# Reordering the start of a Mamba-2 decoder layer: first two units in one explicit order, with PE transposes and PE-spread decays

## The chip, the cores and the metric

The kernel runs on one core of a Trainium2 chip. Its time is device time in microseconds from launch to end; the median of several runs is given. A profile of one execution shows when each instruction ran on each engine: TensorE (PE, with its weight loads as PEld), VectorE (DVE), ScalarE (ACT), GpSimd (POOL), and SyncE (SP), which issues most DMAs.

## The reference: what is computed

Sixteen sequences (batches) of 256 positions and 512 features pass one decoder layer: a Mamba-2 block, a linear-attention block over a context, and a feed-forward block with quantised weights and activations. The change lies in the first. Cut to what matters here:

```python
xz = x @ W_in                              # x after LayerNorm; z 2048, xBC 2048+64+64, dt 32
conv = silu(depthwise_conv4(xBC) + b)      # gives x_conv (32 heads of 64), B (64), C (64)
dt = softplus(dt_proj + dt_bias); A = -exp(A_log)
def step(h, (x_t, dt_t, B_t, C_t)):
    dA = exp(A * dt_t)
    h = dA * h + dt_t * x_t * B_t
    return h, (h . C_t) + D * x_t
y = scan(step); y = y * silu(z); y = y * rsqrt(mean(y*y) + eps); out = y @ W_out
```

## The kernel before: tiles, stages and order

**Pairs and units.** Batches are taken two at a time: eight pairs. In a pair, the 2,048 inner features are taken 128 at a time (two heads): 16 units, so 128 slots of one unit each. The kernel never steps through time. For a unit it multiplies the inputs by a 256x256 matrix of decays times C.B per head, tile by tile of 128 positions. The steps of a unit, with their lines:

- `project_part` (L817): z and x of the unit, for both batches, 12 products each of 128x512 in f16 pairs (hi and lo parts of weight and input, L643).
- `silu_z` (L830), `conv_x` (L836), three taps (`tap_of`, L661), `silu_x` (L845).
- `load_decays` and `load_so_far` (L798, L808): the unit's rows of decays are read from DRAM, the same rows to all 128 partitions, 512 KB and 256 KB per unit.
- `scan` (L851): two VectorE scans make running products of the decays; `cross` (L859) makes the off-diagonal tile.
- `times_g` (L868, L872): multiplies these by G, the masked product C.B of the pair.
- `turn_x` and `x_dt` (L880, L890): x transposed on PE and scaled by dt. `scan_out` (L900, L907): the products with the decay tiles. `plus_dx`, `gated` (L915, L920): y.
- one slot later `split_y`, `squares`, `out_product` (L926, L927, L937, L950): y W_out, summed in four PSUM banks over 16 units.

**What a pair needs first.** `norm_transposed` (L561) makes LayerNorm of a batch, splits it into f16 hi and lo and transposes each by DMA (L624). `time_steps` (L666) makes dt and the decays of all heads, transposes them on PE (L723) and stores them to DRAM (L739, L740). `states` (L744) projects B and C, applies convolution and Silu (L758, L661, L766), copies C from partitions 64 to 127 down to 0 to 63 by DMA (L769), and makes G with six products per batch (L777, L782, L786).

**What pair 0 does besides.** Weights arrive in f32. For each unit `scale_units` (L433) squares them on ACT and derives a power-of-two scale from a PE sum and a chain of six small VectorE instructions; `prepare` (L453) scales on VectorE (wzx, L460), casts on ACT and splits on GpSimd (L464). `wout_make` (L505) does the like for W_out. Units 0 to 9 keep their weights in SBUF; units 10 to 15 share two buffers (`keep_w`, L403): they are prepared in pair 0, stored to DRAM, and later streamed back. So pair 0 takes its units in the order `FIRST` (L107).

**Order.** All engines follow an order that the program writes out itself (`manual_schedule`). A preamble (L1711 to L1771) is written by hand: `step(gen, n)` runs a generator to its n-th `yield`, and the instructions in between go to their engines' queues. Then a loop over slots (L1772) places the unit steps, and between them eight points, `advance(now)` (L1626), at which a small planner places the pieces of background tasks. A task's yield names its wait in points, the allowed points, its engine and its cost; tasks are taken by `rank`, lowest first. `plan` (L1663) starts tasks at given slots. PSUM has one bank for such tasks, given out by `Banks`. In the preamble, unit 0's projections follow batch 1's transposes, decays of units 0 and 1 are loaded, unit 0 is scanned; `times_g` of unit 0 and the rest of `states` (from L769 on) come in slot 1 of the loop (L1816 to L1819). The context for the attention block is made by tasks that `plan` starts in slots 6, 8 and 9.

Of the kernel before, what the change touches and what calls it, by code (L numbers as in the profile page):

```python
# [36 lines left out]
F32 = mybir.dt.float32  # L37
# [10 lines left out]
P = 128  # L48
# [10 lines left out]
def decoder_kernel(  # L59
# [47 lines left out]
    FIRST = (14, 15, 0, 1, 2, 3, 12, 13, 4, 5, 6, 7, 8, 9, 10, 11)  # L107
# [88 lines left out]
    with ExitStack() as part:  # L196
# [84 lines left out]
        class Banks:  # L281
# [8 lines left out]
            def take(self, own=False):  # L290
                me = [own]
                self.line.append(me)
# [25 lines left out]
        def misc(hold, shape, name):  # L318
            ps, tag = (ps_m, "m") if hold == "own" else (ps_p, "proj")
            return ps.tile(shape, F32, tag=tag, name=name)  # L320
# [10 lines left out]
        for j in range(3):  # L331
            nc.scalar.dma_start(bq_sb[32 * j : 32 * j + H, :], bq)
        nc.scalar.dma_start(bk_sb[0:H, :], bk)
# [69 lines left out]
        def keep_w(c, loaded=False):  # L403
# [4 lines left out]
            if not loaded:  # L408
                yield landed(6)
                start(clock[0] // POINTS, scale_units(c, c + 2), rank=-2)  # L410
                start(clock[0] // POINTS, prepare(c + 1), rank=-2)
                yield from prepare(c)
# [20 lines left out]
        def scale_units(c0, c1):  # L433
# [5 lines left out]
            yield pe(0.1)  # L439
            hold = yield from bank.take()  # L440
            pt = misc(hold, [P, c1 - c0], f"ss_ps_{c0}")
            nc.tensor.matmul(pt, ones, ssq_zx[:, c0:c1], start=True, stop=True)
            yield dve(1.2)
# [9 lines left out]
        def prepare(c):  # L453
# [7 lines left out]
            yield act(1.0)  # L461
# [13 lines left out]
        def prepare_bcdt():  # L475
# [14 lines left out]
            scales_from(pt, s, inv_bcdt, "bcdt")  # L490
            for k, (w, cols) in reversed(tuple(enumerate(parts))):
# [68 lines left out]

        def norm_transposed(src, b, what, store):  # L561
# [17 lines left out]
            if b < 2 and what == "m":  # L579
                yield  # L580
                nc.gpsimd.tensor_tensor(rs, rs, mhalf[:, 0:NT], ALU.pow)
                yield
                for i in range(NT):
                    nc.vector.tensor_scalar(
                        y[:, i, :], src[:, i, :], mv[:, i, 0:1], rs[:, i : i + 1],
                        ALU.subtract, ALU.mult,
                    )
                yield
            else:
                nc.vector.tensor_scalar(mv[:, :, 1], mv[:, :, 0], -1.0, None, ALU.mult)  # L590
                yield 1, range(POINTS), "pool", 1.5
                nc.gpsimd.tensor_tensor(rs, rs, mhalf[:, 0:NT], ALU.pow)
                nc.gpsimd.tensor_tensor(mv[:, :, 1], mv[:, :, 1], rs, ALU.mult)
                yield act(2.3, 2)
                for i in range(NT):
                    nc.scalar.activation(
                        y[:, i, :], src[:, i, :], AF.Identity,
                        scale=rs[:, i : i + 1], bias=mv[:, i, 1:2],
                    )
            nc.scalar.copy(hi, y)  # L600
            if b < 2 and what == "m":

                yield
                nc.vector.tensor_tensor(lo, y, hi, ALU.subtract)
            else:
                yield pool(2.4)
                nc.gpsimd.tensor_tensor(lo, y, hi, ALU.subtract)
                yield issued()
# [6 lines left out]
            else:  # L615
                if b % 2 == 0:
                    yield from turned.take()
                    store["lnT"] = [
                        p2.tile([P, 2, NT, KD, P], F16, tag=f"lnT_{n}", name=f"lnT_{n}_m_{b}")
                        for n in "hl"  # L620
                    ]
# [10 lines left out]
        def norm_pair(pair):  # L632
            for j in range(2):
                yield from norm_transposed(None, 2 * pair["k"] + j, "m", pair)
# [13 lines left out]
        def project_pair(dst, w, pair, apart=False, between=None):  # L648

            if apart:  # L650
                for j in range(2):
# [1275 lines left out]
```

## Time and profile before

| what | value |
| --- | --- |
| median of 3 runs | 1966.56 us (1964.16 to 1972.84) |
| profiled execution | 1968.45 us, its span 1966.7 us, mean granted TensorE clock 0.973 |
| PE, DVE, ACT, POOL busy | 1812.7, 1648.8, 1241.2, 720.2 us |
| start of the scans (L851) of units in slots 0, 1, 2, 3, 4 | 47.5, 52.2, 84.1, 95.3, 109.9 us |
| of slots 8, 12, 16 (pair 1) | 170.9, 226.6, 275.0 us |
| of slot 127, the last | 1580.7 us |
| pair 1 to 7, mean per slot | 11.76 us |
| DMA | 360.87 MB, mean 183 GB/s |

The span is what the profiler saw from the first to the last instruction; the execution's time holds 1.75 us more. A slot is best followed by the start of its scan on VectorE, because each unit has exactly one pair of them. The "granted clock" is TensorE's clock in parts of full speed. A line of the timeline reads: start, length, engine, line, operation, output<-inputs, shapes, count, and in brackets how long the engine had been idle and what ended that.

### The profile page before, as it was taken

The numbers are of one execution on the slowest core, as the hardware profiler recorded it, in microseconds if no ns is written. First come the engines' busy times: TensorE is split into PE (matmuls) and PEld (weight loads), VectorE is DVE, ScalarE is ACT, GpSimd is POOL, SyncE is SP. The second block draws the span as 40 slices with busy tenths as digits, with TensorE's granted clock in tenths as the row PEclk, the third lists the DMA queues.
The fourth block names the chain that finished last, engine by engine and source line by source line (L and its number), as shares of the span: only waits on it lengthen the run. The fifth ranks groups of instructions, "written<-read, shape, count | busy, mean of one in ns | idle before, by whom it ended". The sixth has DMA issues, their size and how long they took to land.

```text
span 1966.7 us, 29947 instructions
## 1 busy us (share of the span) xinstructions
PE 1812.7 (92%) x10220; PEld 1040.4 (53%) x10220; DVE 1648.8 (84%) x2705; ACT 1241.2 (63%) x2870; POOL 720.2 (37%) x714
## 2 busy tenths in 40 slices
PE   2687998997999999999999999999999988999998
PEld 2344555654566655566556555655565643444443
DVE  5799986876798888788888898788887878999996
ACT  3665665665677566566766666566656547667775
POOL 2365453333324344565456544343323222100000
PEclk9799999998999999999999999999999999999999
DMA  7555576669758768696578778765858825555454
GB/s 226 152 135 174 160 215 180 187 211 212 208 180 243 222 179 241 201 269 187 160 243 253 180 218 227 212 161 175 221 173 228 235 87 111 120 124 110 113 115 91
DMA packets 301826, 360.87 MB, mean 183 GB/s; under 512 B 168101, under 2 KB 202437, under 8 KB 301674
## 3 DMA queue, kind: packets, MB, share of 16 engines
q1 hardware_dynamic: 282794, 298.10, 57.3%
q0 software_dynamic: 18176, 60.83, 8.7%
q8 instruction: 81, 1.33, 0.3%
q14 instruction: 71, 0.58, 0.1%
q10 hardware_dynamic: 704, 0.04, 0.0%
HBM read 280.47 MB, written 39.58 MB: 163 GB/s over the span
## 4 chain that ended last, share of the span: by engine, by line
PE 63%; DVE 19%; ACT 5%; issue 5%; DMA 4%; POOL 3%; SPq 0%; ACTq 0%; POOLq 0%; DVEq 0%
PE pp L643 23%; PE po L950 13%; PE py L900 5%; PE po_f L1525 4%; PE pu L1484 4%; PE pg L1484 4%; DVE m L851 3%; DVE xs L661 3%; PE trx L880 2%; PE py L907 2%; DVE m L868 1%; ACT xdt L890 1%; DMA wchunk<-in_w_gate_t 1%; DMA ln_m<-in_x 1%; DVE h L1489 1%
## 5 line engine op out<-in xcount | busy, mean ns | idle before, releaser
L643 PE MATMUL pp<-lnT_h_m,w 128*128 128x512 f16 (+1 forms) x2064 | 666.1, 384 | 30.1 <-DVE xs L661 21.0
L643 PEld LDWEIGHTS <-w 128*128 128x128 f16 x3096 | 298.4, 100 | 377.0 <-issue 56.3
L927 POOL TENSOR_TENSOR yl<-y,yh 128x512 fp32r<-128x512 f32 x128 | 172.6, 1349 | 712.2 <-ACT yh L926 657.9
L661 DVE SCALAR_TENSOR_TENSOR xs<-pp,convw_sb,xs 128x510 f32<-128x510 f32 (+2 forms) x384 | 286.2, 745 | 171.4 <-ACT xs L836 162.1
L643 PE MATMUL pp<-lnT_l_m,w 128*128 128x512 f16 (+1 forms) x1032 | 396.0, 384 | 0.0
L890 ACT ACTIVATE xdt<-trx,dt 128x64 f32<-128x64 f32 x1024 | 222.6, 327 | 202.1 <-PE trx L880 201.8
L950 PE MATMUL po<-wout,yh 128*128 128x512 f32 x1024 | 336.7, 410 | 0.2 <-DMA wout<-wout_d 0.2
L851 DVE TENSOR_TENSOR_SCAN m<-dab,starts 128x512 f32<-128x512 f32 x256 | 312.9, 1263 | 0.0
L950 PEld LDWEIGHTS po<-wout,yh 128*128 128x128 f32 x1024 | 183.7, 189 | 56.6 <-ACT sq L937 10.9
L950 PE MATMUL po<-wout,yl 128*128 128x512 f32 x512 | 203.6, 398 | 1.8 <-POOL yl L927 1.8
L845 ACT ACTIVATE xs<-xs 128x512 f32<-128x512 f32 x128 | 80.9, 632 | 193.6 <-DVE xs L661 193.6
L900 PE MATMUL py<-m,xdt 128*64 128x256 f32 x1024 | 163.4, 398 | 20.5 <-ACT xdt L890 12.9
L859 ACT ACTIVATE m<-edb,m 128x128 f32<-128x128 f32 x512 | 164.0, 395 | 16.9 <-DVE m L851 16.5
L1484 PEld LDWEIGHTS <-yT 128*128 128x128 bf16 x1024 | 100.4, 99 | 138.1 <-issue 22.4
L836 ACT ACTIVATE xs<-pp,convb_sb,convw_sb 128x512 f32<-128x512 f32 x128 | 100.1, 782 | 108.3 <-PE pp L643 108.2
L938 POOL TENSOR_TENSOR ssq<-ssq,sq 128x512 f32<-128x512 f32 x120 | 155.8, 1298 | 33.5 <-ACT sq L937 32.7
L868 DVE TENSOR_TENSOR m<-m,g 128x1024 f32<-128x1024 f32 x128 | 161.6, 1263 | 0.1
L1484 PE MATMUL pg<-w_ffn,yT 128*128 128x512 bf16 x512 | 133.2, 383 | 8.5 <-ACT h L1488 5.6
L1484 PE MATMUL pu<-w_ffn,yT 128*128 128x512 bf16 x512 | 133.2, 383 | 5.8 <-DVE x L976 5.1
L1488 ACT ACTIVATE h<-pg,sg 128x512 f32<-128x512 f32 x128 | 86.7, 682 | 75.9 <-PE pg L1484 75.7
L1525 PE MATMUL po_f<-w_ffn,hT 128*128 128x512 bf16 x512 | 127.4, 383 | 4.8 <-DMA hT<-hq 4.8
L950 PEld LDWEIGHTS po<-wout,yl 128*128 128x128 f32 x512 | 96.7, 189 | 27.9 <-POOL yl L927 4.6
(261 smaller groups left out, 2856.5 us busy)
## 6 DMA issues: line engine op xcount, KB each, us to landing
dab<-da_d SPq DMA_DIRECT2D x128, 512.0 KB
wout<-wout_d SPq DMA_DIRECT2D x112, 512.0 KB
edb<-ed_d SPq DMA_DIRECT2D x128, 256.0 KB
w<-w_d SPq DMA_DIRECT2D x40, 512.0 KB
w<-in_w_zx SPq DMA_DIRECT2D x16, 512.0 KB
wout_d<-wout SPq DMA_DIRECT2D x16, 512.0 KB
ctxT<-in_ctx_t POOLq DMA_DIRECT2D x16, 512.0 KB, 8.0
x<-in_x SPq DMA_DIRECT2D x16, 512.0 KB
```

What stands on the lines that cost most here:

```text
L643: nc.tensor.matmul(dst, w(wi, kc), yT[yi][:, :, kc, :], start=n == 0, stop=n == 3 * KD - 1)
L661: nc.vector.scalar_tensor_tensor(u[:, :, d:S], raw[:, :, 0 : S - d], w[:, j : j + 1], u[:, :, d:S], ALU.mult, ALU.add,)
L851: nc.vector.tensor_tensor_scan(u["m"][:, 4 * j : 4 * j + 4, :].rearrange("p k t -> p (k t)"), u["da"][:, j].rearrange("p h i t -> p (h i t)"),
L859: nc.scalar.activation(u["m"][:, 8 + n, :], u["ed"][:, n // 2, n % 2, :], AF.Copy, scale=u["m"][:, 2 * n, P - 1 : P],)
L868: nc.vector.tensor_tensor(m, m, gi.unsqueeze(2).to_broadcast([P, 2, 2, NT * P]), ALU.mult)
L890: nc.scalar.activation(u["xdt"][:, j, i, h, :], u["tr"][:, j, i, h * HD : (h + 1) * HD], AF.Copy, scale=dt[:, i, j, 2 * c + h : 2 * c + h ...
L900: nc.tensor.matmul(py[h * HD : (h + 1) * HD, j, :].rearrange("p (i t) -> p i t", i=NT), xdt[:, j, 0, h, :], m[:, 2 * (2 * j + h) : 9 + 2 * ...
L927: nc.gpsimd.tensor_tensor(lo, u["y"], hi, ALU.subtract)
L938: nc.gpsimd.tensor_tensor(pair["ssq"], pair["ssq"], sq, ALU.add)
L950: nc.tensor.matmul(pair["po"][n], u["yhl"][yi][:, j, i * P : (i + 1) * P], w[:, wi, :], start=c == 0 and p == 0, stop=c == NU - 1 and p == 2,)
L1484: nc.tensor.matmul(dst, yT[:, kc, :], w_ffn[w + kc][:, cols], start=kc == 0, stop=kc == KD - 1)
L1525: nc.tensor.matmul(u["po"], u["hT", k // (KF // 2)][:, k % (KF // 2), :], w_ffn[2 * KD + k // NF][:, (k % NF) * D : (k % NF + 1) * D], sta ...
```

## The change

The preamble and slots 0 and 1 are written out in one order, and the loop starts at slot 2. In it:

- Batch 0 is loaded as two tiles. `norm_first` replaces `norm_transposed` for batches 0 and 1: f32 transposes on PE into PSUM, four per tile of 128 positions; hi is cast out of PSUM on ACT, lo subtracted on VectorE.
- `spread_decays`: for unit 0 the decay rows, in SBUF after `time_steps`, are spread over all partitions by PE products with a repeated column of the identity; the DMA loads of unit 0's decays go, those of unit 2 come in their place.
- Unit 1's projections follow unit 0's directly; `states` goes on to the C copy (L769) in the preamble, and G follows before unit 0's `times_g`.
- All ten resident weights are requested before the first LayerNorm; units 0 to 3 get their scales in one chain.
- Four small DMAs of the query and key biases go from ACT's queue to GpSimd's.
- In `plan`: units 12 and 13 move one place back in `FIRST`, unit 4 two places forward; context constants start in slot 10 (before 6), query weights in 14 (8), the first context in 12 (9). Several ranks and waits change. Batch 3 of pair 1 gets a buffer of its own.

The diff, cut to its core:

```diff
-    FIRST = (14, 15, 0, 1, 2, 3, 12, 13, 4, 5, 6, 7, 8, 9, 10, 11)
+    FIRST = (14, 15, 0, 1, 2, 3, 4, 12, 13, 5, 6, 7, 8, 9, 10, 11)
...
-            nc.scalar.dma_start(bq_sb[32 * j : 32 * j + H, :], bq)
-        nc.scalar.dma_start(bk_sb[0:H, :], bk)
+            nc.gpsimd.dma_start(bq_sb[32 * j : 32 * j + H, :], bq)
+        nc.gpsimd.dma_start(bk_sb[0:H, :], bk)
...
+        def norm_first(y, b, pair):
...
+            pts = []
+            for i in range(NT):
+                pt = ps_o.tile([P, KD, P], F32, tag=f"o{NT * b + i}", name=f"ln_t_{b}_{i}")
+                pts.append(pt)
+                for kc in range(KD):
+                    nc.tensor.transpose(pt[:, kc, :], y[:, i, kc * P : (kc + 1) * P], ident)
+                nc.scalar.copy(hi[:, b, i], pt)
+            yield
+            for i in range(NT):
+                nc.vector.tensor_tensor(lo[:, b, i], pts[i], hi[:, b, i], ALU.subtract)
+            yield
...
+        def spread_decays(u):
...
+                    for i in range(NT):
+                        one = 2 * NH * i + row
+                        nc.tensor.matmul(
+                            u["da"][j][:, h, i, :], ident[:, one : one + 1].to_broadcast([P, P]),
+                            pair["da_t"], start=True, stop=True,
+                        )
...
-                start(s, time_steps(pair), rank=-1)
+                start(s, time_steps(pair), rank=-1 if k else -5)
...
-                elif s == 1:
-                    start(s, keep_w(12), rank=-2)
+                elif s == 2:
+                    start(s, keep_w(12), rank=-3)
                 elif s == 7:
-                    start(s, keep_w(10), rank=-2)
+                    start(s, keep_w(10), rank=-3)
...
-                if c == 6:
+                if c == 10:
                     start(s, context_constants())
-                elif c == 8:
+                elif c == 14:
                     start(s, queries_weights(), 1, 2)
-                elif c == 9:
+                elif c == 12:
                     start(s, context_pair(0), 1, rank=1)
...
+        for c in range(NRES):
+            load_w(c)
...
+        step(norm1)
+        step(prep1)
+        pair["ready", "m"] = True
+        project_part(u0, 0, of=0)
+        step(steps_)
+        step(scale1, 3)
+        project_part(u0, 0, of=1)
+        project_part(u0, 1)
...
+        step(steps_, 2)
+        step(scale1, 2)
+        conv_x(u0)
+        step(scale1)
+        step(steps_, 3)
+        step(scale1)
+        step(states_, 2)
+        step(prep2, 2)
+        step(steps_, 3)
+        step(prep2)
+        for n in (1, 2):
+            u = units[n] = units.get(n) or unit(n)
             load_decays(u)
             load_so_far(u)
+        spread_decays(u0)
         silu_z(u0)
-        conv_x(u0)
+        step(states_, 3)
         for j in (2, 1, 0):
             tap(u0, j)
         silu_x(u0)
-        step(states_, 4)
-        step(scales_[1], 5)
+        step(prep2)
+        project_part(u1, 0)
+        plan(0)
+        advance(1)
         scan(u0)
         cross(u0)
-        for s in range(n_slots + 3):
+        turn_x(u0)
+        x_dt(u0)
+        silu_z(u1)
+        advance(2)
+        project_part(u1, 1)
+        conv_x(u1)
+        advance(3)
+        drive(states_)
+        times_g(u0)
+        for j in (2, 1, 0):
+            tap(u1, j)
+        silu_x(u1)
+        plan(1)
+        advance(8)
+        scan_out(u0)
+        scan(u1)
+        cross(u1)
+        advance(9)
+        plus_dx(u0)
+        gated(u0)
...
+        for s in range(2, n_slots + 3):
...
-            if s == 1:
-
-                drive(states_)
-                times_g(u1)
```

## The prediction

> **What bounds the kernel now.** I read the shares of busy time first: TensorE (PE) is busy 92% of the span, so 154 us without a matmul are spread over 1,966.7 us. The 40 slices put the holes at the front. So I took the busy time in stretches (columns: stretch, its length, then PE, PEld, DVE, ACT, POOL busy with instruction counts, granted clock, DMA share, GB/s):
>
> ```profile
> 40.00:50.00 10.00, 0.59 (x2) 0.50 (x2) 5.57 (x12) 4.22 (x9) 0.00 (x0) 0.65 0.56 153
> 50.00:60.00 10.00, 5.42 (x16) 2.78 (x17) 9.89 (x11) 6.92 (x17) 7.39 (x4) 0.50 0.87 215
> 60.00:70.00 10.00, 3.25 (x16) 1.30 (x14) 2.44 (x5) 6.87 (x14) 5.51 (x4) 0.84 0.93 339
> 70.00:80.00 10.00, 6.66 (x31) 5.03 (x32) 6.38 (x15) 0.00 (x0) 1.43 (x3) 0.50 0.14 18
> ...
> 130.00:145.00 15.00, 13.35 (x113) 8.29 (x111) 14.96 (x9) 8.79 (x22) 14.32 (x10) 1.00 0.61 130
> ```
>
> Between 40 and 80 us PE has 15.9 us of work and VectorE 24.3; nothing is full. From 130 on VectorE is. The chain that ended last, in order of time (start, length, what), says what the early stretch waits for:
>
> ```profile
> 61.22 8.64 DMA cT<-bcT
> 69.99 1.63 PE pg L777 x6
> 72.42 1.63 PE pg L777 x6
> 74.69 1.13 DVE m L868
> ```
>
> That is the copy of C to partitions 0 to 63 (L769), the six products C.B per batch (L777), and the first multiplication of decays by them (L868), which every unit needs. Why so late? SyncE's timeline: the decays of units 0 and 1 are asked for at 41.7, C only at 61.2, though its Silu (L766) had ended at 43.64:
>
> ```profile
> 41.69 0.39 SPq L798 DMA_DIRECT2D dab<-da_d  x1
> 42.18 0.41 SPq L808 DMA_DIRECT2D edb<-ed_d  x1
> 42.64 0.46 SPq L798 DMA_DIRECT2D dab<-da_d  x1
> 43.16 0.70 SPq L808 DMA_DIRECT2D edb<-ed_d  x1
> ...
> 61.22 0.59 SPq L769 DMA_DIRECT2D cT<-bcT  x1
> ```
>
> L769 stands in slot 1 behind loads that wait for VectorE. From 82 to 275 us the 14 remaining slots of pair 0 take 13.65 us each (first scan at 84.1, pair 1's at 275.0) against 11.76 later; VectorE is busy 186.2 of the 200 us from 75 to 275. So whatever brings the first L868 forward shifts a full VectorE stretch, and behind it a full PE stretch: it reaches the end one for one unless that stretch gets longer.
>
> **Part 1: LayerNorm turned on PE.** Before, batch 1's hi and lo go through two transposing DMAs: lo is written at 23.25, its DMA issued at 23.28, PE gets it at 26.60, and the time-step products L678 end at 27.4. Now: 16 PE transposes (the row trx x4 is 0.63 us for four; 2.5 us in all), four ACT copies out of PSUM at about 0.65 (L830, 128x512 out of PSUM: 0.69) and four VectorE subtractions at about 0.65 (L604 is 1.23 for twice the width). Batch 1 is normalised at about 18.3 (before 20.5; its statistics follow batch 0's at once), turned by 20, copied by 20.5, split by 21.8. Then 12 products of 256 columns for batch 0 (0.21 each cold, 2.5), of which 1.3 lie ahead of the split, and the 48 of L678 (1.3): 24.7 instead of 27.4, **2.7 gained**. Bounds: nothing, if the ACT queue (now with the weight casts and squares between the copies) is late by as much; 6 if PE is warm and nothing queues. Pushed later in SyncE's order is batch 1's load: before, the ninth DMA (L391) waited until the first (alog) landed at 6.1; now that load is ninth. Half a megabyte at the 390 GB/s of that stretch lands by about 10, its reader comes at 12.9: hidden; uncovered it would cost up to 4. The ten weight loads now issue before 20 us instead of until 28.7; they read in what was idle DMA time and end by about 28.
>
> The Trainium skill ("Advanced Engine Details and Errata", X-Bar Transpose) speaks against this part: a transposing DMA on trn2 is to be as fast as a plain one. The trace agrees: 3.3 us from issue to use here, against a 4.5 us median for the plain 256 KB loads of L508. By the rule the only thing to win is the latency of a DMA, not a slow transpose; the sum above counts just that.
>
> **Part 2: decays by PE.** VectorE's chain L692 to L736 was 8.05 us (27.41 to 35.46). Inserted ahead of its end are one scale chain (1.0) and one wzx (0.75), of which 0.76 fills the wait for the transpose: da_t ends at 35.46 - 2.7 + 1.0 = 33.8. Unit 0's decays then need 12 products instead of a DRAM round trip. No row has such an f32 product with 128 columns and 128 rows; the nearest are L777 (64 rows, 0.14 warm, 0.27 cold) and, from above, L900 (256 columns, half the columns of PE, mean 0.64 cold). So 1.7 to 7.7; I take 3, near L777. The unit 0 scan can run at 38 instead of 47.5, but **it is not on the path**: its reader L868 waits for C. If I am off by all of 4.7, that still ends before C.
>
> The skill ("FP8 and Floating Point Precision", TensorE Precision Notes) counts four passes for a true f32 product, which would be about 2.6 us warm and 5.1 cold for the twelve, as an estimate. Neither moves the sum, for the same reason.
>
> **Part 3: C earlier, unit 1 right behind.** SyncE now has da_d x2, ed_d, then decays of units 1 and 2 (again 2 x 768 KB), then cT. Stores to first load took 35.49 to 41.69, 6.2 us; so loads issue at 33.8 + 6.2 = 40.0 and cT at about 42 (bcT's Silu ends at 36.5, so it does not wait for that). Before, 1.5 MB of broadcasts drained from 42.0 to about 50.2; so they end at 48.3 and cT at 48.5. Bounds: from its own issue plus a 4.5 us median landing, 46.5; plus the 8.64 us of before, 50.6. From there 4.7 us, as before (69.99 to 74.69, at a granted clock of 0.50, which I keep since PE idles from about 42; 3.2 warm by L777's and L782's rows): first L868 at **53.2 instead of 74.6, 21.4 earlier** (bounds 19 to 25).
>
> Then the stretch to slot 2's first instruction (L868 of unit 1, at 82.36 before). Before it held 7.75 us. Now: L868 and L872 of unit 0 (1.8), unit 1's taps (2.3), its scan (2.3, which before lay at 52 to 56), L915 and L920 (1.45), statistics of batch 2 (2.1), one wzx (0.75): 10.7. Slot 2 starts at 53.2 + 10.7 = 63.9: **18.5 earlier**. PE's part of unit 1 (24 products, 0.215 apart warm, 0.42 cold before) lies before 42, under the wait for C.
>
> **Part 4: rest of pair 0.** The same instructions in another order: context constants from slot 6 to 10, query weights 8 to 14, context pairs 9 to 12, units 12 and 13 one slot later, unit 4 earlier. VectorE's sum is unchanged: 0. Context results were written at 452 us, slot 31, and pair 1 asks for them in slot 34; if they miss that, two batches take the store-and-reload path: 2 MB, about 11 us of DMA at the mean 183 GB/s, beside everything else on queues that the page shows 57% and 9% busy. Bounds of part 4 come from VectorE's own rows: the same two scans take
>
> ```profile
> 136.43 5.29 DVE L851 TENSOR_TENSOR_SCAN m<-dab,starts 128x512 f32<-128x512 f32 x2
> ...
> 151.16 2.33 DVE L851 TENSOR_TENSOR_SCAN m<-dab,starts 128x512 f32<-128x512 f32 x2
> ```
>
> and at 136 GpSimd is in unbroken tensor_tensor work (14.32 of 15 us), at 151 it is idle. Mean minus shortest over the stretch: scans 28 x 0.28, L868 16 x 0.20, L920 15 x 0.37, L511 13 x 0.33, L460 10 x 0.40, about 25 us, with single inflated small ones about 35 us that VectorE loses while both run. A new order can raise or lower this by some 10 either way; I have no row that favours a side.
>
> **Sum.** Profiled execution 1,968.45 (1.75 outside its span), less 18.5: 1,950. The median of the runs shown, 1,966.56, lies 1.9 under the profiled one, so **1,948**. Likeliest case alone: 18.5 with -10 to +12 of parts 1, 3 and 4: 1,936 to 1,957.
>
> **Rivals.**
> A, given back at units 10 and 11 (0.14). Their loads wait until unit 13 is used. Before: loaded at 154 (slot 7), GpSimd's split from 242.7, first use on PE at 247.5: 93 us of chain with 2.6 to spare. Unit 13 is now used one slot later while unit 10 stays in slot 14. If the chain stays 93 us, PE waits 13.65 - 2.6 = 11 us: 1,959. Against it: that chain now has a better rank (-3 instead of -2) and the first place at the bank, and 93 us hold only some 10 us of its own instructions.
> B, slower (0.06). One mechanism: VectorE and GpSimd collide more in slots 2 to 15. The 35 us lost there must grow by more than 18.5 to cancel; if it doubles, 1,948 + 35 = 1,983. For it: with unit 1 brought forward, three splits of weights (2.1 each) and three of W_out (1.3) fall beside the scans. Against it: GpSimd is busy only 103 of 200 us, and no work is added to it but four small DMA issues at the start.
> C, collisions fall by half as much (0.08): 1,948 - 17 = 1,931.
> D, the shift is real but C does not come early (0.04): the loads of units 1 and 2 wait longer for the stores, cT lands at 60 and the gain is 7: 1,960.
> The forecast has 0.68.
>
> **Chances and range.** What this kernel's measurement can tell from no change is about 0.5%, 9.8 us: below 1,956.7 is faster. Forecast and C: 0.76 faster. A and D, same: 0.18. B: 0.06 slower. The range 1,934 to 1,961 holds forecast, A and D and leaves out C and B, 0.14, and a little of the forecast's tails.
>
> **What would show it.** Right: L678 ending near 24.7; cT issued near 42, landed by 50; first L868 at 51 to 56; unit 2's first scan at 64 to 69 instead of 84.1; pair 1's first scan near 256 instead of 275; 11.8 us per slot after that. Wrong: L868 early but pair 1's first scan at 265 or later (A shows as PE idle before slot 14, B as scans above 2 us); or cT still behind the broadcasts at 55 and later, which would show that the queue, and not the order of issue, set its time.

## The result, and the profile after

The changed kernel takes **1,993.12 us** (median of 9 runs, 1,979.59 to 1,998.83), the kernel before 1,972.84 in 9 runs beside it: **ratio 1.010, 95% interval 1.0069 to 1.0132**. The forecast of 1,948 was wrong, and on the wrong side. The profiled execution is 1,997.74, its span 1,996.0, the mean granted clock 0.968.

Line numbers have moved: L643 is now L665, L661 L682, L678 L699, L723 L744, L769 L791, L777 L799, L798 L821, L808 L831, L851 L896, L868 L913, L950 L995, L567 L603 and L624 L641. The same stretches as before (columns as there: PE, PEld, DVE, ACT, POOL busy, granted clock, DMA share, GB/s):

```profile
40.00:50.00 10.00, 9.18 (x34) 4.44 (x34) 5.25 (x8) 4.99 (x16) 0.00 (x0) 0.75 0.96 187
50.00:60.00 10.00, 4.99 (x24) 4.02 (x26) 5.03 (x9) 0.93 (x1) 2.12 (x1) 0.60 0.47 185
60.00:70.00 10.00, 7.85 (x38) 3.47 (x35) 9.83 (x15) 9.81 (x24) 7.04 (x6) 0.89 0.59 138
70.00:80.00 10.00, 6.17 (x29) 4.26 (x30) 9.48 (x16) 5.38 (x10) 5.89 (x4) 0.83 0.84 243
...
130.00:145.00 15.00, 9.26 (x90) 5.82 (x87) 14.72 (x19) 6.61 (x18) 8.39 (x7) 0.86 0.32 105
```

The hole at the front is much smaller: between 40 and 80 PE has 28.2 us of work instead of 15.9. The chain still goes through the copy of C, G and the first multiplication, but earlier:

```profile
40.79 10.74 DMA cT<-bcT
51.66 1.41 PE pg L799 x6
...
53.87 1.63 PE pg L799 x6
...
56.06 1.22 DVE m L913
```

SyncE's timeline shows C asked for at 40.79 instead of 61.2, still behind four loads of decays, and 2.83 us in issue:

```profile
38.50 0.39 SPq L821 DMA_DIRECT2D dab<-da_d  x1
39.13 0.38 SPq L831 DMA_DIRECT2D edb<-ed_d  x1
39.55 0.46 SPq L821 DMA_DIRECT2D dab<-da_d  x1
40.07 0.62 SPq L831 DMA_DIRECT2D edb<-ed_d  x1
40.79 2.83 SPq L791 DMA_DIRECT2D cT<-bcT  x1
```

So the front did about what it should, and the time still grew. To see where, I set the start of each slot's scan (L896) against before's (L851): slot 2 starts at 69.8, 14.3 us **earlier**; slot 16 is 7.5 earlier, slot 33 7.2 earlier; slot 88 is 18.1 **later** and slot 112 27.6 later. From slot 127 to the end both need 386 to 388. The loss lies in slots 33 to 112, where the diff changes no instruction, only the order of tasks. Two stretches from slot 40 to 112, first of before, then of after:

```profile
576.80:1420.40 843.60, 818.47 (x4878) 496.28 (x4876) 717.71 (x1057) 545.96 (x1397) 397.10 (x383) 0.99 0.75 211
```

```profile
564.80:1448.00 883.20, 833.78 (x4918) 505.81 (x4917) 733.12 (x1063) 546.73 (x1396) 407.33 (x387) 0.97 0.74 203
```

After needs 39.6 us more. PE idles 49.4 instead of 25.1 us (length less busy: 24.3 of the 39.6). It is also busy 15.3 longer: it has 40 products more here, about 7 us at 0.17 each, and its granted clock is 0.97 instead of 0.99. The waits of after in slots 56 to 111 (engine, tile, line <- what ended the wait: us, times, longest) have entries that before's same slots lack. L610 is the statistics of a later batch's LayerNorm, L995 the product with W_out, L1082 a product of the attention block, L699 the time-step products:

```profile
DVE ln_st_m L610 <- DMA ln_m<-in_x: 15.1, 2, 10.6
...
PE po L995 <- DMA wout<-wout_d: 10.8, 2, 6.3
...
PE pa L1082 <- ACT zs L875: 8.1, 2, 6.3
...
PE pd L699 <- DMA lnT_h_m<-lnh_m: 4.8, 1, 4.8
```

x, W_out and transposed tiles land late. Two parts of the diff reach that far: who takes the PSUM bank of the tasks first (`take(first=True)`, in every pair), and the slots in which `plan` starts the context tasks. The first two runs try the second part alone.

### The profile page after: what moved, and what is told of

Same layout as the page of the kernel before. It is cut to its first block, busy times and chain, and to the rows that moved or that the text cites. A ratio compares the mean times of both kernels' runs of the same rounds, so it can differ in the third digit from the quotient of the medians.

```text
span 1996.0 us, 29966 instructions
## 1 busy us (share of the span) xinstructions
PE 1834.8 (92%) x10246; PEld 1051.0 (53%) x10246; DVE 1667.8 (84%) x2701; ACT 1240.8 (62%) x2872; POOL 728.1 (36%) x718
## 4 chain that ended last, share of the span: by engine, by line
PE 53%; DVE 24%; DMA 7%; issue 5%; ACT 5%; POOL 4%; SPq 1%; POOLq 0%; ACTq 0%; DVEq 0%
PE pp L665 17%; PE po L995 10%; PE pu L1529 5%; PE po_f L1570 5%; PE pg L1529 5%; DVE m L896 4%; DVE xs L682 4%; PE py L945 3%; DVE m L913 2%; PE trx L925 2%; DMA lnT_l_m<-lnl_m 2%; PE py L952 1%; ACT xdt L935 1%; DVE sp_q L731 1%; DVE m L917 1%
## 5 line engine op out<-in xcount | busy, mean ns | idle before, releaser
L665 PE MATMUL pp<-lnT_h_m,w 128*128 128x512 f16 (+1 forms) x2056 | 664.2, 384 | 31.0 <-DVE xs L682 21.7
L665 PEld LDWEIGHTS <-w 128*128 128x128 f16 x3084 | 296.9, 99 | 376.7 <-issue 59.6
L682 DVE SCALAR_TENSOR_TENSOR xs<-pp,convw_sb,xs 128x510 f32<-128x510 f32 (+2 forms) x384 | 286.2, 745 | 174.7 <-ACT xs L881 165.3
L665 PE MATMUL pp<-lnT_l_m,w 128*128 128x512 f16 (+1 forms) x1028 | 394.9, 384 | 0.0
L995 PE MATMUL po<-wout,yh 128*128 128x512 f32 x1024 | 341.8, 415 | 10.8 <-DMA wout<-wout_d 10.8
L896 DVE TENSOR_TENSOR_SCAN m<-dab,starts 128x512 f32<-128x512 f32 x254 | 305.1, 1242 | 3.2 <-DMA dab<-da_d 3.2
L995 PEld LDWEIGHTS po<-wout,yh 128*128 128x128 f32 x1024 | 187.1, 193 | 68.4 <-issue 20.3
L995 PE MATMUL po<-wout,yl 128*128 128x512 f32 x512 | 205.9, 402 | 5.0 <-POOL yl L972 4.9
L904 ACT ACTIVATE m<-edb,m 128x128 f32<-128x128 f32 x508 | 162.8, 397 | 12.8 <-DVE m L896 11.3
L913 DVE TENSOR_TENSOR m<-m,g 128x1024 f32<-128x1024 f32 x128 | 162.5, 1270 | 0.1
L995 PEld LDWEIGHTS po<-wout,yl 128*128 128x128 f32 x512 | 98.4, 192 | 32.8 <-POOL yl L972 9.1
## 6 DMA issues: line engine op xcount, KB each, us to landing
ctxT<-in_ctx_t POOLq DMA_DIRECT2D x16, 512.0 KB, 10.4
```

The source lines that it names most:

```text
L665: nc.tensor.matmul(dst, w(wi, kc), yT[yi][:, :, kc, :], start=n == 0, stop=n == 3 * KD - 1)
L682: nc.vector.scalar_tensor_tensor(u[:, :, d:S], raw[:, :, 0 : S - d], w[:, j : j + 1], u[:, :, d:S], ALU.mult, ALU.add,)
L896: nc.vector.tensor_tensor_scan(u["m"][:, 4 * j : 4 * j + 4, :].rearrange("p k t -> p (k t)"), u["da"][j].rearrange("p h i t -> p (h i t)") ...
L904: nc.scalar.activation(u["m"][:, 8 + n, :], u["ed"][:, n // 2, n % 2, :], AF.Copy, scale=u["m"][:, 2 * n, P - 1 : P],)
L913: nc.vector.tensor_tensor(m, m, gi.unsqueeze(2).to_broadcast([P, 2, 2, NT * P]), ALU.mult)
L995: nc.tensor.matmul(pair["po"][n], u["yhl"][yi][:, j, i * P : (i + 1) * P], w[:, wi, :], start=c == 0 and p == 0, stop=c == NU - 1 and p == 2,)
```

## The experiments

A measure that serves for all of them is the **loss from slot 33 to 112**: how much the start of scan 112 falls behind that of scan 33, against before's distance. Both ends have nearly the same tasks behind them; in between the two orders differ in what is already done, so leads there compare only roughly. All in us, from one profiled execution each. Six of the kernels have the same first two slots (after, e1, e9, e10, f1, f2); their slot 2 starts at 67.1 to 69.8, so a difference of 3 us there is within what single profiles differ by, and the medians with their intervals decide:

| kernel | slot 2 | slot 16 | slot 33 | slot 112 | loss 33 to 112 | median (ratio) |
| --- | --- | --- | --- | --- | --- | --- |
| after | -14.3 | -7.5 | -7.2 | +27.6 | 34.8 | 1993.1 (1.0100) |
| e1 contexts at 11 | -15.0 | -7.4 | -5.2 | +2.9 | 8.1 | 1968.2 (0.9982) |
| e2 before, contexts at 12 | +0.1 | +0.9 | +3.0 | +32.3 | 29.3 | 1991.4 (1.0109) |
| e3 = e1, C first | -21.3 | -13.7 | -11.4 | -13.4 | -2.0 | 1963.3 (0.9946) |
| e4 = e1, no spread | -18.8 | -11.3 | -10.1 | +0.3 | 10.4 | 1963.5 (0.9950) |
| e5 = after, x on GpSimd's queue | -10.7 | -3.9 | -4.4 | +24.6 | 29.0 | 1993.9 (1.0106) |
| e6 = e3, x on GpSimd's queue | -21.6 | -13.8 | -12.5 | -9.1 | 3.4 | 1958.2 (0.9928) |
| e7 = e3 and e4 | -15.7 | -8.9 | -7.3 | -9.1 | -1.8 | 1960.8 (0.9946) |
| e8 = e1, turned by DMA | -6.5 | +0.8 | +2.5 | +10.8 | 8.3 | 1978.1 (1.0028) |
| e9 = e1, batch 1 held | -15.7 | -8.0 | -5.7 | +13.1 | 18.8 | 1985.3 (1.0072) |
| e10 = after, batch 1 early | -15.2 | -6.7 | -5.1 | +17.0 | 22.1 | 1985.9 (1.0067) |
| e11 = e6, pair 3 earlier | -19.6 | -12.7 | -11.5 | -9.3 | 2.2 | 1957.8 (0.9928) |
| e12 = e10 with C first and x | -17.0 | -13.6 | -12.5 | +1.9 | 14.4 | 1973.5 (1.0006) |
| f1 = after, W_out kept | -17.0 | -13.5 | -13.1 | -2.6 | 10.5 | 1972.7 (0.9995) |
| f2 = e1, W_out kept | -14.9 | -6.8 | -5.1 | -5.0 | 0.1 | 1963.6 (0.9960) |

The 95% intervals of the ratios, in the order of the table from e1 on: 0.9967 to 0.9997, 1.0069 to 1.0149, 0.9925 to 0.9966, 0.9932 to 0.9968, 1.0079 to 1.0133, 0.9904 to 0.9951, 0.9927 to 0.9965, 1.0014 to 1.0043, 1.0050 to 1.0094, 1.0044 to 1.0089, 0.9908 to 0.9947, 0.9986 to 1.0026, 0.9965 to 1.0026, 0.9944 to 0.9976.

**The start slot of the contexts.** The theory: the later start alone makes the slowdown. Two kernels, one with everything but it, one with nothing but it.

The first diff is e1, on after; the second e2, on before.

```diff
-elif c == 12:
+elif c == 11:
     start(s, context_pair(0), 1, rank=1)
```

```diff
-elif c == 9:
+elif c == 12:
     start(s, context_pair(0), 1, rank=1)
```

> The changed kernel with one number altered: the first context pairs start in slot 11 instead of 12. Read off the instruction lists, this alone puts every background task from slot 16 on into the slot it had before the change (batch 0's attention norm in slot 35 instead of 39, pair 3's LayerNorm in 46 and 49 instead of 51 and 54). Theory S (the loss is the later schedule of background tasks, whose in-order consumers then meet late DMAs; the new start itself gains): unit 2's first scan near 70 as in the changed kernel, pair 1's first scan 7 to 12 us ahead of before, and that lead is kept to the last scan; time 1957 to 1965, 25 to 35 us under the changed kernel. Theory P (the new start costs by itself, for instance through a lower clock or colliding VectorE and GpSimd): lead lost again between slots 36 and 112, time 1980 or more.

> The kernel before with one number altered: the first context pairs start in slot 12 instead of 9; its start is untouched. By the instruction lists its background tasks then lie in the same slots as in the changed kernel. Theory S: no difference up to slot 12, then 25 to 40 us lost between slots 36 and 112; time 1990 to 2010, and PE waits there for loads of W_out, transposes and z. Theory P: within 5 us of before, 1962 to 1975.

In the main both as the theory had it: 1,968.2 and 1,991.4. The start at slot 12 costs some 20 us by itself, as much as the whole change, and with the start one slot earlier this loss is gone. Not as expected, e1's lead is not kept: of 7.4 us at slot 16 nothing is left at slot 34, and the time lies 3 us above theory S's range. A planner places the tasks, and it jumps between two orders: written out, the starts at 9 and 11 give one order of the later tasks, 12 another, in which the first contexts are worked out two slots later, LayerNorm of pair 4 five slots later, and batch 1, which waits in DRAM for the contexts, is done with its attention at slot 88 instead of 64. (Pairs are counted from 0 here: what the expectations call pair 3's LayerNorm in e1 and pair 2's second x in e6 belongs to pairs 4 and 3.)

**The front.** With most of the late loss out of the way (e1), the parts of the front can be told apart.

The first diff is e3, the second e4, both on e1; e7 has both edits.

```diff
+step(states_, 3)
 for n in (1, 2):
...
 spread_decays(u0)
 silu_z(u0)
-step(states_, 3)
```

```diff
-for n in (1, 2):
-    u = units[n] = units.get(n) or unit(n)
-    load_decays(u)
-    load_so_far(u)
-spread_decays(u0)
+units[2] = unit(2)
+for n in (0, 1):
+    load_decays(units[n])
+    load_so_far(units[n])
...
 scan(u0)
+load_decays(units[2])
 cross(u0)
+load_so_far(units[2])
```

> As e1_ctx11, and the copy of C is issued ahead of the decay loads of units 1 and 2 instead of behind them; nothing else moves. If the queue in front of it set C's landing (51.5 in the changed kernel, issued 40.8): C is issued near 39.2 and lands by 44, the first multiplication by G comes at 48 to 50 instead of 56, and unit 2's first scan at 63 to 66; time 4 to 6 us under e1_ctx11. If the DMA of C itself takes its 8 to 11 us wherever it stands: landing at 48 to 50, gain 2 at most.

> As e1_ctx11, but unit 0's decays come by DMA from DRAM as before and unit 2's are loaded after unit 0's scan; the twelve spreading products go. If the spread is off the path, as the prediction had it (unit 0's scan can run at 48 without delaying the multiplication by G): first multiplication by G within 1.5 us of the changed kernel's 56.1, time within 3 us of e1_ctx11. If it matters: scan of unit 0 after 48, and the VectorE work behind it pushes the multiplication by G to 58 or later, 3 to 6 us slower.

> The two edits of the front together: contexts at slot 11, C's copy issued first, and no decays spread by TensorE products (units 0 and 1 take theirs by DMA, behind C). If the queue ahead of C is all that set C's landing, the first multiplication of decays by G comes as early as with C first alone, slot 2 starts at 62 to 64 us (62.8 and 65.3 with one edit each) and the time is that of the two, 1,960 to 1,964. If the twelve spread products and what they delay on TensorE (5.8 us at 36 to 42) still count with C in front, slot 2 starts 3 us earlier, at 59 to 60, and up to 3 us are gained. If unit 0's decays, now behind C in the queue, become the last thing awaited, slot 2 starts at 66 or later and the time is 1,966 or more.

In e3 the copy of C stands ahead of the decays. The chain in e1, then SyncE's timeline and the chain in e3:

```profile
39.63 10.97 DMA cT<-bcT
50.74 1.63 PE pg L799 x6
```

```profile
39.12 0.48 SPq L791 DMA_DIRECT2D cT<-bcT  x1
```

```profile
45.24 0.88 PE pg L799 x6
```

C's products start 6.1 us after the issue instead of 11.1 in e1 (39.63 to 50.74), slot 2 6.3 us earlier than in e1. So what stands ahead in the queue delays C's landing. It is not all that does: with C first its products start 6.0 to 6.1 us after the issue in e3, e6 and e11, but 8.1 in e7 and 8.8 in e12; with C behind the decays it is 10.1 to 11.4 in the six profiles of the same front. Without the spread (e4) slot 2 comes 3.8 earlier than in e1, and the median is 4.7 lower: C is issued at 38.84 and its products start at 47.66, 8.8 later, though the loads ahead of it are of the same size. What differs is behind it: in e1 two stores of weights and two loads of x are issued from 42.47 on, in e4 the loads of unit 2's decays wait in front of them until 43.8. That these share the DMA engines with C is argued from the order of issue and was not tried alone. So what I called off the path costs some 4 us; whether by the products or, as the landing suggests, by the order of the loads, no run parts. Both edits together (e7) bring slot 2 less far forward than either: 68.4, because unit 0's scan now waits 5.36 us for decays that stand behind C, as the third case of its expectation said (its time was not: 1,960.8 instead of 1,966 or more).

e8 puts the old way into `norm_first`, on e1:

```diff
-        nc.tensor.transpose(pt[:, kc, :], y[:, i, kc * P : (kc + 1) * P], ident)
-    nc.scalar.copy(hi[:, b, i], pt)
-    nc.vector.tensor_tensor(lo[:, b, i], pts[i], hi[:, b, i], ALU.subtract)
+nc.scalar.copy(hi16, y)
+nc.vector.tensor_tensor(lo16, y, hi16, ALU.subtract)
+for t, part_ in zip((hi, lo), (hi16, lo16)):
+    nc.sync.dma_start_transpose(
+        t[:, b].rearrange("p i k t -> p (i k) t"), part_.rearrange("p i d -> p (i d)")
+    )
```

> Contexts at slot 11, and the first part alone undone: batches 0 and 1 are turned by transposing DMAs again (hi copied by ScalarE, lo subtracted by VectorE, two transposes per batch on SyncE's queue) instead of on TensorE. If the turn on TensorE is worth what its direct chain shows, the time-step products end at 27 to 28 us instead of 23.3 and slot 2 starts 3 to 5 us later, at 72 to 74 instead of 69.1. Rival: the weights of the first units (scales, casts and splits) and the order on the engines set the front, and slot 2 moves by under 1.5 us. A second rival: the four transposes get in front of the ten weight loads in SyncE's queue, nothing waits for these, and the decays are no later. The time itself, 1,968 with the turn on TensorE, should move by under 5 us, since a lead of that size has been lost again in slot 33.

The time-step products end at 33.5 instead of 24.2 in e1 (23.3 in after), later even than in before (27.4), and slot 2 8.6 later than in e1; 7.9 of that are still there at slot 112, and the median is 9.9 higher. None of these sizes was expected: batch 0's transposes now stand behind ten weight loads and issue slowly, as SyncE's timeline has it:

```profile
16.98 4.58 SPq L592 DMA_TRANSPOSE lnT_h_m<-lnh_m  x1
21.67 4.09 SPq L592 DMA_TRANSPOSE lnT_l_m<-lnl_m  x1
```

So with weight loads this early the turn on PE is worth 8 to 10 us; transposes issued ahead of those loads were not tried. The Trainium skill ("Advanced Engine Details and Errata", X-Bar Transpose) has a transposing DMA on trn2 as fast as a plain one; the 3.3 us from issue to use in before agree with that, but it says nothing of the issue itself, which behind ten loads of 512 KB these rows show.

**What is late in slots 33 to 112.** First the queue:

The same edit for e5, on after, and e6, on e3:

```diff
-nc.sync.dma_start(y, x[b].rearrange("(i p) d -> p i d", p=P))
+nc.gpsimd.dma_start(y, x[b].rearrange("(i p) d -> p i d", p=P))
```

> The changed kernel with one edit: from pair 2 on, the load of x for a batch's first LayerNorm (line 603) is issued on GpSimd's queue instead of SyncE's, where it stands behind the transposing DMAs of the batch before. Theory Q (what comes late in the new order of tasks comes late because SyncE issues in order and its transposes take 3 to 8 us to issue when transfers meet): the two waits of VectorE for ln_m in slots 56 to 108 (15.1 us) go, W_out, which stands in the same queue, is issued a little earlier, and the time falls by 8 to 16 us, to 1,977 to 1,985. Theory D (the 16 DMA engines are full in those slots, whatever queue asks): x lands as late as before, the waits move to W_out or stay, and the time stays within 5 us of the changed kernel's 1,993.

> The kernel with C first (contexts at slot 11, C's copy issued ahead of the decay loads) with the same edit: x of the later batches on GpSimd's queue. It took 31.2 us from scan 33 to scan 34, with 16.1 us of VectorE waiting for pair 2's second x, issued at 477 behind two transposes of 12.8 and 10.9 us. Theory Q: x is issued at about 455, lands by 470, scan 33 to 34 takes 18 to 21 us and the time falls from 1,963 to about 1,951. Theory D: x lands at about 480 all the same, scan 33 to 34 stays at 28 us or more, 1,960 or more.

The edit also moves the load of batch 2 (pair 1). The waits for x in slots 56 to 111 of e5 are gone, and the time is the same, 1,993.9: the wait for W_out grew from 10.8 to 14.0 us. In e6 x is asked for at 452.3, 19.0 us before it lands; scan 33 to 34 takes 30.3 instead of 31.2. Its gain over e3 (1,958.2 against 1,963.3) is within their intervals. Theory Q falls as the cause of the late loss.

Then which batches meet. The first diff is e9, on e1; the second e10, on after. e12 is e10 with e3's and e6's edits.

```diff
+while b in (1,) and clock[0] < 60 * POINTS:
+    yield WAIT
+while b in (4, 5) and clock[0] < 82 * POINTS:
+    yield WAIT
 yield from late.take()
```

```diff
-yield from lns.take(rank=0 if what == "m" else 2 if "late" in store else 1)
+yield from lns.take(rank=0 if what == "m" else 0 if b < 2 else 2 if "late" in store else 1)
...
-yield from attends.take(rank=2 if waits else 1)
+yield from attends.take(rank=0 if b < 2 else 2 if waits else 1)
...
+while b in (4, 5) and clock[0] < 82 * POINTS:
+    yield WAIT
 yield from late.take()
```

> Contexts at slot 11 (the old order of tasks; 1,968, its slots 56 to 112 take 651.9 us against 696.3 in the changed kernel), with one task held: batch 1, which waits in DRAM for the contexts, is reloaded for its attention only from slot 60 on (as the changed kernel does: 60, attention at 81) instead of 54, so that its LayerNorm and attention lie among those of batches 6 and 7 in slots 61 to 83; batches 4 and 5 follow from slot 82. Theory B (three batches' attentions in slots 66 to 83 instead of two, with their transposes, stores and loads, are what makes TensorE's inputs late in the changed kernel): slots 66 to 88 take 15 to 25 us longer than with contexts at slot 11 and the time rises to about 1,985. Rival K (it is the whole row of later tasks, the next contexts and LayerNorms two to five slots later, that meets badly, and batch 1 is only one of them): under 6 us, 1,974 at most.

> The changed kernel (contexts at slot 12) with batches 0 and 1 put first in the lines for LayerNorm, transposed tiles and attention, so that batch 1 is reloaded at slot 52 and done at 63 instead of 60 and 88, and batches 4 and 5 held until slot 82. Two batches instead of three have their attention in slots 66 to 83; the next contexts and LayerNorms stay as late as in the changed kernel. Theory B: the stretch from slot 66 to 88 gets 15 to 25 us shorter, the time 1,970 to 1,980. Rival K: at most 6 us, 1,987 or more.

> All together on the changed kernel (contexts at slot 12): batch 1 early and batches 4 and 5 held as in the run before, C's copy issued ahead of the decay loads, x of later batches on GpSimd's queue. Slot 2 starts at 62 to 63 us instead of 69.8, slot 34 at about 480 (no stall at 33, as in the changed kernel). With theory B the late loss goes as well and the time is 1,950 to 1,960; with rival K it comes back to the changed kernel's less the 6 to 7 us of C first, about 1,985.

Holding batch 1 in the old order, with batches 4 and 5 behind it, brings the time that theory B said, 1,985.3, 17 more than e1 (10.2 by slot 112 in the profile); slots 66 to 88 take 11.4 us longer, less than B's 15 to 25. The opposite edit gains 7.2 by the medians, with intervals that overlap, and 12.7 of the loss in the profiles, and not where B put it: from slot 64 to 88 after falls back 24.5 us against before, e10 23.7. So crowded attentions are a way to lose 10 to 17 us, but not all that is wrong with the new order. e12 fits neither of its two theories: 1,973.5, with a loss of 14.4, and its slot 2 starts at 67.1 instead of 62 to 63.

e11, on e6, starts pair 3's LayerNorm one slot earlier:

```diff
-if (s == 1 or c == NU - 3) and k + ahead < NP:
+if (s == 1 or c == (NU - 4 if k == 1 else NU - 3)) and k + ahead < NP:
```

> The kernel with C first and x on GpSimd's queue (1,958; 30.3 us from scan 33 to 34), with the LayerNorm of pair 3 started one slot earlier, so that its first batch is transposed at about 438 us, before GpSimd asks for 1.5 MB of contexts, three chunks of FFN weights and another 1 MB at 449 to 460. Theory: transposes that meet those loads take 12.6 and 11.7 us to issue, and that is what holds scan 34; out of their way they take under 3 us each, scans 33 to 35 take 25 us or less instead of 39, and the time falls to about 1,945. Rival: the loads themselves are awaited (TensorE waits for the contexts 6 to 12 us there), the second batch's transposes meet the FFN chunks one slot later, and 33 to 35 stays above 34 us, 1,955 or more.

This concerns a stall that before has too: scan 33 to 34 takes 30.8 us there, 17.2 in after. In e6 two transposes meet the loads of contexts and of FFN weights on SyncE's queue; one slot earlier (e11) they do not. First e6, then e11:

```profile
449.61 12.57 SPq L641 DMA_TRANSPOSE lnT_h_m<-lnh_m  x1
462.28 11.72 SPq L641 DMA_TRANSPOSE lnT_l_m<-lnl_m  x1
```

```profile
445.77 1.30 SPq L641 DMA_TRANSPOSE lnT_h_m<-lnh_m  x1
447.17 2.68 SPq L641 DMA_TRANSPOSE lnT_l_m<-lnl_m  x1
```

The issue fell as the theory had it, scan 33 to 34 to 20.1 us, scans 33 to 35 from 38.9 to 29.4, between theory and rival, and the time did not move (1,957.8): of 9 us at slot 34, 2.3 are left at slot 40 and nothing at 112. Where the rest was lost again stays open.

Last, less to load: f1, on after, and f2, on e1, with one edit.

```diff
 def wout_load(b, c):
-    t = p2.tile([P, 2, D], F32R, tag="wout", name=f"wout_{b}_{c}")
-    nc.sync.dma_start(t.bitcast(F32), wout_d[c])
-    return t
+    if "kept" not in wouts:
+        t = wouts["kept"] = p2.tile([P, 2, D], F32R, tag="wout", name=f"wout_{b}_{c}")
+        nc.sync.dma_start(t.bitcast(F32), wout_d[c])
+    return wouts["kept"]
```

> The changed kernel without the reload of W_out: from pair 1 on every unit multiplies by the same tile of W_out (that of pair 1's first unit), so 512 KB less are loaded per slot, some 44 of the 205 GB/s that the late slots move; the instructions of all engines stay. Read beside its twin in the old order of tasks. Theory D (the late loss is full DMA engines: in the new order more transfers meet, and W_out, transposed tiles and x land late): with this room both orders run alike, the two differ by under 8 us instead of 25, and this one takes 1,955 to 1,970. Rival E (tasks of the engines themselves meet, in the in-order queues of ScalarE, VectorE and TensorE, and the DMA waits are only where it shows): only the 10.8 us of waits for W_out and part of the clock lost after them go, 1,975 to 1,985, and the two still differ by 15 us or more.

> The twin: contexts at slot 11 and W_out not reloaded from pair 1 on (every unit multiplies by pair 1's first tile). With the old order of tasks TensorE waits for W_out only in slot 33 to 35 (2.6 us), and in that stall transposes meet the contexts' loads. Theory D: a few us less in slot 33 to 34, 1,955 to 1,965. Rival E: 1,965 or more, no change.

The two kernels leave out the reload, so their output is not the layer's; they serve the time alone. Slots 40 to 112, first f1, then f2, then e1, which f2 is to be read beside as f1 beside after:

```profile
556.40:1417.80 861.40, 824.88 (x4918) 499.50 (x4917) 732.94 (x1062) 545.48 (x1396) 405.60 (x387) 0.99 0.65 164
```

```profile
573.70:1415.40 841.70, 817.11 (x4878) 495.98 (x4876) 718.95 (x1057) 545.90 (x1397) 397.15 (x383) 0.99 0.65 167
```

```profile
577.10:1423.20 846.10, 819.72 (x4878) 496.89 (x4877) 717.57 (x1056) 545.82 (x1397) 396.65 (x383) 0.99 0.75 211
```

With some 40 GB/s less to move (164 against 203), the new order gets 20 us faster and the old one 5; the difference of the two falls from 24.9 us to 9.1 (medians), from 26.7 to 10.4 in the loss from 33 to 112. With f1's interval of 6 us either way, theory D's "under 8" is not excluded and rival E's "15 or more" lies at the edge: **about 16 of the 25 us, give or take several, hang on the reload of W_out.** Its bytes are one thing that goes with it; its place in SyncE's queue and PE's waits for W_out itself (10.8 us) go too, and no run parts them. The mean load does not tell the two orders apart: the DMA share is 0.74 in after and 0.75 in before and e1, 0.65 in f1 and f2. That the transfers of the new order meet at worse moments is therefore the likely reading, but argued. The other 9 stay without W_out's reload; f1 still waits for x (9.3 us), for transposed tiles (4.5 and 5.7 us for lnT_h) and for ScalarE's zs (7.0). What exactly they are is open.

## Why the prediction was wrong

- **Part 1, right in kind.** L699 ends at 23.3 (forecast 24.7), 4.1 us gained instead of 2.7. With the early weight loads beside it, it is worth more: e8 says 8.6 at slot 2.
- **Part 2, end of da_t: 33.8 forecast, 35.95 measured** (L757, as L736 ended the chain of before). I counted a scale chain on VectorE and missed that PE's twelve products for B and C stand ahead of the transpose of da and wait for that chain's small reads of PSUM, then run partly at a low clock (granted 0.62 from 30.5 to 35.0). PE's and VectorE's timelines:

```profile
30.50 0.38 PE L665 MATMUL bc<-lnT_h_m,w_bc 128*128 128x512 f16 x1 [2.71 <-DVE ss_t_zx L369]
```

```profile
35.08 0.29 DVE L747 COPY da_t<-pda 128x128 f32<-128x128 f32 x1 [3.08 <-PE pda L744]
...
35.89 0.06 DVE L757 MEMSET da_t<- 128x1 f32 x1
```

- **The spread**: 36.01 to 41.8, 5.8 us instead of 3, inside the bounds 1.7 to 7.7. The sum took twelve rows of the trace for twelve products. In the trace each of these f32 products stands as two rows: twelve products in the code are 24 rows (L848 x16, L853 x8), about 0.11 us apart while the granted clock is 1.00 (36.0 to 37.6) and 0.21 while it is 0.50 (38.6 to 41.8). The row it was priced by, L777 x6, is likewise three products per batch in the code, not six. Priced by product, L777 would have given 3.4 to 6.5. The Trainium skill's four passes ("FP8 and Floating Point Precision", TensorE Precision Notes) gave an estimate of 5.1 cold, nearer than the row I took. That the spread lies off the path holds for its products as far as the chain shows (L913 waits for C); yet e4, without it and with the loads in another order, is 3.8 us earlier at slot 2.
- **Part 3.** Loads issue at 38.5 (40.0), C at 40.8 (42). That they are not late is luck: da_t was 2.2 late, but from the stores to the first load it took 2.5 us instead of the 6.2 that I kept from before. C then lands at 51.5, not 48.5, and beyond the bound of 50.6. I bounded its landing by a plain load and by its old time; that it shared the engines with more is likely, and not shown alone. First L913 at 56.06 instead of 53.2. The stretch to slot 2 is 12.0 (forecast 10.7). Slot 2's first instruction comes 14.3 us earlier instead of 18.5: 2.9 lost on C's way, 1.3 in the stretch.
- **Part 4 is the step that failed**: "The same instructions in another order: ... VectorE's sum is unchanged: 0", with bounds of 10 either way. Two things were in it. In pair 0 half of the lead goes: 14.3 at slot 2, 7.5 at slot 16, with VectorE busy 182.8 instead of 177.4 us there; that is like rival B at a fifth of its size, and within the bounds. And the contexts' start, which I priced by a store-and-reload path of two batches (it is the same four reloads in both kernels), costs 20 us by e2 (25 between after and e1) through the order of tasks 20 to 100 slots later. I looked for what the moved tasks cost and for when their result is needed; not at what the planner does with all that follows them. No rival covered that.
- **"It reaches the end one for one unless that stretch gets longer"** was too simple also without it: e1 is 15.0 earlier at slot 2 and 0.4 later at slot 40: 7.6 went in pair 0 and 5.6 between slots 33 and 40, in a stall of the old order that before has as well and that is longer in e1 (36.7 us from scan 33 to 34 instead of 30.8). Of e3's 21.3, 13.4 arrive at slot 112 of its profile, 8.2 in the medians.

The scan beside GpSimd that before showed at 5.29 us is not inflated in after:

```profile
136.98 2.33 DVE L896 TENSOR_TENSOR_SCAN m<-dab,starts 128x512 f32<-128x512 f32 x2
```

Of the collisions of after, the last section shows one with smaller instructions.

The sum by medians: all with the contexts' start at slot 11 (e1) is -3 us, the start at 12 alone (e2) +20; the change has +20. What e1 could have gained and did not, e3, e6 and e11 show, which beat both kernels: 1,963 us with the copy of C first and contexts at slot 11, and **1,958 us, 0.993 of before**, with x on another queue besides, though that last step lies within the intervals.

## What to carry to other kernels

When a planner places the later work, moving the start of one task is a change to everything behind it: write out both orders and compare where batches, loads and transposes meet, before calling it zero. In this kernel a lead at the front was worth only what the later stalls let through, so read the DMA share and PE's idle time there first. And a short copy that the critical chain needs goes to the queue ahead of half-megabyte loads, not behind them.

## What the runs showed of the hardware

A transposing DMA takes 1.3 us to issue in e11, where GpSimd asks for 1 MB of loads from 441 to 450 us, and 12.6 in e6, where it asks for 3.75 MB in the 11 us around it (rows above). SyncE's next DMA follows only at 474.1 in e6, behind both transposes.

VectorE's instructions take longer where GpSimd's work lies beside them, and a small shift in time decides whether the two meet. After and f1 have the same instructions in pair 0, yet f1 is 6.0 earlier at slot 16: 2.7 at slot 2 already, and 3.7 appear in slot 7. There GpSimd's subtraction starts just before two VectorE instructions in after, and after them (138.33) in f1. VectorE in after, GpSimd in after, VectorE in f1:

```profile
139.85 1.23 DVE L720 SCALAR_TENSOR_TENSOR sp_v<-sp_r,sp_v 128x128 f32<-128x128 f32 x1
141.01 2.60 DVE L460 TENSOR_SCALAR wzx<-w,s_zx 128x1024 f32<-128x1024 f32 x1
```

```profile
139.65 1.29 POOL L972 TENSOR_TENSOR yl<-y,yh 128x512 fp32r<-128x512 f32 x1 [6.03 <-ACT yh L971]
140.90 2.16 POOL L464 TENSOR_TENSOR w<-wzx,w 128x1024 f16<-128x1024 f32 x1
```

```profile
137.65 0.29 DVE L721 SCALAR_TENSOR_TENSOR sp_v<-sp_r,sp_v 128x128 f32<-128x128 f32 x1
137.86 0.75 DVE L460 TENSOR_SCALAR wzx<-w,s_zx 128x1024 f32<-128x1024 f32 x1
```

In after the two take 3.8 us instead of 1.0, and PE then waits 5.75 us for the scale behind them (2.0 in f1). That GpSimd's work is the reason rests on these two single profiles. Differences of under 6 us between two single profiles of this kernel are weak evidence; the intervals above are better.
